# A planned four-layer graph network on one core: transposes in TensorE's planned gaps, fewer one-column products, and wider lags between the layers

## The chip, the core and the metric

The kernel runs on one core of a Trainium2 chip. A core has five engines that each work through a queue of their own, in order: TensorE (PE, matrix products and transposes), VectorE (DVE), ScalarE (ACT), GpSimd (POOL) and SyncE (SP, which here only issues DMAs). They wait for each other through semaphores. The metric is the device time of one execution in microseconds. Before the change it was 1075.67 us, the median of three runs (1072.64 to 1078.02).

## What is computed

The input x is 32 batches of 512 nodes with 128 features; adj is one 512x512 matrix of zeros and ones, shared by all batches. Four graph layers follow each other, each on a normalized copy of x and with a residual:

```python
h = jnp.maximum(_layernorm(x, axis=-1), 0.0);  x = x + L0(h, adj, ...)
h = jnp.maximum(_layernorm(x, axis=-1), 0.0);  x = x + L1(h, adj, ...)
h = jnp.maximum(_layernorm(x, axis=-1), 0.0);  x = x + L2(h, adj, ...)
h = jnp.maximum(_layernorm(x, axis=-1), 0.0);  x = x + L3(h, adj, ...)
```

- Layer 0 is an attention whose scores need only a few values per node (the index arithmetic of the reference pairs nodes up), with a softmax over the first axis, plus a product with a second weight.
- Layer 1 is an attention over edges, multiplied by adj, then a normalization, a sum over neighbours, and a small two-layer network with its own normalization.
- Layer 2 is an attention over edges with an ELU behind it.
- Layer 3 multiplies by a fixed 512x512 matrix, the same for all batches: a softmax over the weights e, which are handed out to the edges of adj in the order in which the edges are counted. That matrix is worked out once (the edge numbers come from cumulative sums, done as products).

All is in 32-bit floats.

## The kernel before

All of x stays on the chip (`xs`). A batch in a layer is one *chain* of operations: statistics of a row (L494, L496, DVE), the power that gives the inverse deviation (L508, POOL), the normalization `xn` (L543, POOL), a transpose of four blocks (L405, PE), a ReLU into `hT` (L553, ACT), products with the weights (`proj` L578, or `p` L564), and then what the layer needs. Layers 1 and 2 share `attend`: `prow` (a transpose that repeats a row), score plus mask with the row maximum (L605, DVE), leaky ReLU and exponential (L630, L638, ACT), transposes of y, `pT` (L647 or L398), and the products `po` (L658). Layer 0 has its own form with pairs of scores fetched by small DMAs (`u`), two scaled copies of h (`hs`, `hs2`, L788 and L789, DVE), a difference `hl` (L803, POOL) and the products L817 to L830. Layer 3 has `own` (L952, DVE), `p`, a copy of h (L396, ACT), the products L963 and L967, the addition `yo` (L974) and the store (L975).

Two chains stand beside those of the batches: `prepare` (masks, centred weights, rows) and `prepare_last` (layer 3's matrix: `pn`, `pb`, `pk`, `pg`, `e_at`, `pd`, `offT`).

The order of the work is written by a planner (`Plan`). Each operation is registered with its engine, a length, its inputs and its outputs; `run` then plays the whole program through with these lengths and a fixed delay per engine. At each step it takes, over all engines, the ready operation that can begin first. Among operations of one engine that can begin within `SLACK` of each other it takes the one with the lowest *turn*. The turn of an operation is its chain's begin plus `STRETCH` times the length of the way to it within its chain; the two preparing chains have a first turn and a step for each operation instead (`PREPARED`, `FILLED`). The begin of a chain is the sum of the gaps (`GAPS`, one for each layer) of the chains ahead of it; the first `AHEAD` = 6 gaps are multiplied by `RAMP`. `LAGS` says by how many batches each layer follows layer 0. A chain may run only within a window of 20 chains from the oldest unfinished one, and a chain at `OLD` or more places from the oldest leaves `KEPT` buffer of a room free. The rooms stand for the 8 banks of PSUM and for groups of SBUF buffers. The engines then follow the planned order on the chip, each at its own pace: a queue never overtakes.

Of the kernel before, what the change touches and what calls it, by code (L numbers as in the profile page):

```python
# [28 lines left out]
F32 = mybir.dt.float32  # L29
# [4 lines left out]
AF = mybir.ActivationFunctionType  # L34
ALU = mybir.AluOpType
AX = mybir.AxisListType

P = 128
# [3 lines left out]

WINDOW = 20

OLD, KEPT = 3, 1

AHEAD = 6

# [1 line left out]
PE, DVE, ACT, POOL, SP = "PE", "DVE", "ACT", "POOL", "SP"  # L50
# [6 lines left out]

SLACK = 0.05

STRETCH = 4.0  # L60

PREPARED, FILLED = (40.0, 1.0), (150.0, 1.5)

RAMP = 4.0

GAPS, LAGS = (5.7, 12.9, 7.2, 5.8), (0, 4, 9, 12)


class Room:
# [38 lines left out]
class Plan:  # L108
# [4 lines left out]
    def __init__(self, tc):  # L113
        self.tc = tc
        self.ops = []
        self.chains = []
        self.begin = 0.0

    def chain(self, gap=0.0, beside=None, name=""):

# [32 lines left out]
    def run(self):  # L153
        tc, nc = self.tc, self.tc.nc
        idle = dict.fromkeys(DELAY, 0.0)
        bus = 0.0
        lanes = [0.0] * LANES

        held = {DVE: [], POOL: []}
        ready = {e: [] for e in DELAY}  # L160
        for op in self.ops:
            if not op.missing:
                ready[op.engine].append(op)
        left = [c[0] for c in self.chains]
        normal = [k for k, c in enumerate(self.chains) if c[1] is None]
        order = {k: i for i, k in enumerate(normal)}
        oldest = 0
        last = {}
        traced = nc.cur_bb.bb.instructions
        seen = len(traced)  # L170
        for _ in range(len(self.ops)):
            while oldest < len(normal) and not left[normal[oldest]]:
                oldest += 1
            best = None
            for engine, ops in ready.items():
                could = []
                for op in ops:
                    k = op.chain
                    beside = self.chains[k][1] is not None
                    if not beside and order[k] >= oldest + WINDOW:  # L180
                        continue
                    begin = max(idle[engine], op.ready)
                    if op.transfers:
                        begin = max(begin, lanes[op.transfers - 1])
                    if op.port:
                        for a, b in held[POOL if engine is DVE else DVE]:
                            if a <= begin < b:
                                begin = b
                    new = [s for s in op.slots if s.tile is None]
                    rooms = {}  # L190
                    for s in new:
                        rooms[s.room] = rooms.get(s.room, 0) + 1
                    for room, n in rooms.items():
                        if len(room.free) < n + (room.reserve if beside else KEPT if order[k] >= oldest + OLD else 0):
                            begin = None
                            break
                        begin = max(begin, sorted(room.free)[n - 1])
                    if begin is not None:
                        could.append((begin, op.turn, op))
                if could:  # L200
                    first = min(c[0] for c in could)
                    c = min((c for c in could if c[0] <= first + SLACK), key=lambda c: c[1])
                    if best is None or c[0] < best[0]:
                        best = c
            assert best is not None, "no operation can begin"
            begin, _, op = best
            ready[op.engine].remove(op)
            for s in op.slots:
                if s.tile is None:
                    s.room.free.remove(min(s.room.free))  # L210
                    s.tile = s.room.make(s.name)
            end = begin + op.length
            idle[op.engine] = end
            if op.port:
                piece = op.length / op.port
                held[op.engine] = [(begin + k * piece, begin + (k + 1) * piece - HOLD) for k in range(op.port)]
            done = end + DELAY[op.engine]
            if op.load:
                bus = max(done, bus) + op.load
                done = bus  # L220
            if op.transfers:
                lanes = lanes[op.transfers :] + [done] * op.transfers
            op.emit()
            traced = nc.cur_bb.bb.instructions
            while seen < len(traced):
                ins = traced[seen]
                seen += 1
                if ins.engine in last:
                    tc.add_manual_dep(
                        ins, last[ins.engine].name,  # L230
                        mybir.DependencyInfo(mybir.DependencyClass.NoSync, mybir.DependencyReason.DATA),
                        reason="the plan's order",
                    )
                last[ins.engine] = ins
            left[op.chain] -= 1
            for s in op.slots:
                s.users -= 1
                s.until = max(s.until, done)
                if not s.users:
                    s.room.free.append(s.until)  # L240
            for n in op.after:
                n.missing -= 1
                n.ready = max(n.ready, done)
                if not n.missing:
                    ready[n.engine].append(n)
# [3 lines left out]
def kernel(  # L249
# [28 lines left out]
    nc = tc.nc  # L278
    B, N, F = x.shape
    C = N // P  # L280
# [4 lines left out]
    KE = NE // P  # L285
# [16 lines left out]
    def const(name, shape, dtype=F32):  # L302
        return cp.tile(list(shape), dtype, name=name)
# [6 lines left out]
    banks = Room(8, lambda n: ps.tile([P, C, P], F32, tag="bank", name=n), reserve=2)  # L310
# [7 lines left out]

    plan = Plan(tc)
    op = plan.op  # L320

    def value(r, name):
        return Value(Slot(r, name))
# [112 lines left out]
    edge = []  # L436
# [7 lines left out]
            wide(e.t).bitcast(BF16)[:, 0:N], bias[:, ib, :], 0.0, None, ALU.is_gt), [v_adj[ib]], [e])  # L444
        edge.append(e)

    def count():
        for jb in range(C):
            for hf in range(2):
                for k in range(H):  # L450
                    nc.tensor.matmul(
                        counts.t[:, jb, hf : hf + 1], lhsT=wide(edge[hf * H + k].t).bitcast(BF16)[:, blk(jb)],
                        rhs=one_b, start=(k == 0), stop=(k == H - 1),
                    )

    op(PE, 1.2, count, edge, [counts])

    def no_edges():

# [23 lines left out]
    def dve(length, emit, reads, writes, port=0):  # L483
        op(DVE, length, emit, reads, writes, port=port)
# [569 lines left out]
    def prepare_last():  # L1054
# [14 lines left out]
        def bf_t():  # L1069
            return wide(bf.t)[:, 0 : 2 * P]  # L1070
# [46 lines left out]
                [pn], [v_n])  # L1117
        pb = value(banks, "pb")

        def emit_pb():  # L1120
            for ib in range(C):
                for kb in range(ib + 1):
                    nc.tensor.matmul(
                        pb.t[:, 0, ib : ib + 1], lhsT=bf_t()[:, 0:P] if kb == ib else bf_t()[:, P:],
                        rhs=row_n[:, kb : kb + 1], start=(kb == 0), stop=(kb == ib),
                    )

        op(PE, 2.2, emit_pb, [bf, v_n], [pb])

        def emit_lo():  # L1130
            nc.vector.tensor_copy(row_lo, pb.t[:, 0, 0:C])
# [45 lines left out]
        def e_at_t(t, kb):  # L1177
            return wide(e_at[t][kb].t).bitcast(F32R)
# [1 line left out]
        in_rowT = [*parts(spare, "in_rowT", 1), *parts(spare, "in_rowT", 1)]  # L1180
        pk = value(banks, "pk")

        def emit_pk():
            for kb in range(KE):
                for ib in range(C):
                    nc.tensor.matmul(
                        pk.t[:, 0, kb : kb + 1], lhsT=in_row_t(ib)[:, blk(kb)], rhs=row_lo[:, ib : ib + 1],
                        start=(ib == 0), stop=(ib == C - 1),
                    )

        op(PE, 1.75, emit_pk, [*in_row, v_lo], [pk])
        dve(0.15, lambda: nc.vector.scalar_tensor_tensor(
            first_k, pk.t[:, 0, 0:KE], -1.0, next_k, ALU.mult, ALU.add), [pk, v_next], [v_first])
        for kb in range(KE):
# [18 lines left out]

            op(POOL, 1.4, emit_at, [ge], [v_adiag_rep], port=1)

            def emit_e(kb=kb):
                for t, e in enumerate((e_hi.bitcast(F32), e_lo)):
                    nc.vector.tensor_scalar(e_at_t(t, kb), adiag_rep, e[:, kb : kb + 1], None, ALU.mult)

            dve(0.65, emit_e, [v_adiag_rep, v_terms], [e_at[0][kb], e_at[1][kb]])  # L1220
            pt = value(banks, "pt_row")
            turn_op(lambda k, pt=pt: pt.t[:, k, :], lambda k, kb=kb: in_row_t(k)[:, blk(kb)], in_row, [pt])
            copy_op(ACT, 0.59, lambda kb=kb: wide(in_rowT[kb].t).bitcast(F32R), lambda pt=pt: wide(pt.t),
# [5 lines left out]
        for ib in range(C):  # L1229
# [32 lines left out]

            def emit_div(ib=ib):
                a = offT[:, ib, :]
                nc.vector.reciprocal(rsum3[:, ib : ib + 1], sum3[:, ib : ib + 1])
                nc.vector.tensor_scalar(a, a, rsum3[:, ib : ib + 1], None, ALU.mult)

            dg = value(spare, "dg")

# [7 lines left out]
            op(POOL, 1.25, emit_mask, [v_bias], [share[ib]], port=1)  # L1277
            dve(0.8, emit_first, [pd], [share[ib]])
            op(ACT, 0.8, emit_exp, [], [share[ib]])
            dve(0.5, emit_div, [], [share[ib]])  # L1280
            dve(0.72, emit_diag, [], [share[ib], dg, v_diag[ib]])
        turned3 = [value(banks, "pt_att3") for _ in range(C)]
        for jb, pt in enumerate(turned3):
# [54 lines left out]
```

## Time and profile before

| | |
|---|---|
| median of three runs | 1075.67 us |
| profiled execution | 1077.78 us |
| its span, first to last instruction | 1076.0 us |
| instructions | 24957 |
| PE busy | 1045.5 us, 97% of the span |
| PE weight loads busy | 965.0 us, 90% |
| DVE busy | 871.7 us, 81% |
| POOL busy | 796.4 us, 74% |
| ACT busy | 763.4 us, 71% |
| mean granted TensorE clock | 0.980 |

A product in 32-bit floats is shown as two instructions (two passes), a transpose as one. Busy times of groups overlap where instructions are pipelined, so that the mean of one is more than what it costs in a row of many. The chain that ended last is PE for 85% of the span. The profile gives the granted clock of PE as a share of its full speed; in the first microseconds it says 1.00, though the transposes there take as long as others do at 0.50.

### The profile page before, as it was taken

How to read it: one execution, taken by the hardware profiler on the slowest of the kernel's cores; microseconds unless marked ns; L12 is line 12 of the kernel's file. 1: busy time of each engine (PE TensorE's matmuls, PEld its weight loads, DVE VectorE, ACT ScalarE, POOL GpSimd, SP SyncE). 2: the span in 40 equal slices, each digit the busy share in tenths (PEclk: the TensorE clock that was granted, in tenths of full speed). 3: DMA queues.
4: the chain of work that ended last, by engine and by line, in shares of the span. 5: the costliest groups of instructions: out<-in, count | busy, mean ns of one | idle time of the engine just before them, and what ended most of it. 6: DMA issues, size and time to landing. Idle time of an engine off the chain costs nothing.

```text
span 1076.0 us, 24957 instructions
## 1 busy us (share of the span) xinstructions
PE 1045.5 (97%) x8341; PEld 965.0 (90%) x8341; DVE 871.7 (81%) x3702; ACT 763.4 (71%) x1976; POOL 796.4 (74%) x1176
## 2 busy tenths in 40 slices
PE   6999999999999999999999999999999999999996
PEld 5887789899899999999999999999999999999995
DVE  7798999999887888888888888888788787776562
ACT  4466778887776777787777777777777777776561
POOL 8689756879777778877787787778778777657644
PEclk8698999999999999999999999999999999999998
DMA  7300000000000000000000000000000000000000
GB/s 179 76 11 1 2 2 10 12 12 21 2 21 21 21 21 22 21 1 21 22 21 12 11 12 4 9 11 12 11 11 12 11 11 12 11 11 21 11 26 25
DMA packets 56912, 20.48 MB, mean 19 GB/s; under 512 B 21584, under 2 KB 56272, under 8 KB 56784
## 3 DMA queue, kind: packets, MB, share of 16 engines
q1 hardware_dynamic: 56784, 18.90, 7.2%
q8 instruction: 66, 1.08, 0.4%
q14 instruction: 62, 0.51, 0.2%
HBM read 10.43 MB, written 8.39 MB: 17 GB/s over the span
## 4 chain that ended last, share of the span: by engine, by line
PE 85%; POOL 5%; DVE 5%; issue 2%; ACT 1%; DMA 1%; SPq 0%; POOLq 0%; DVEq 0%; ACTq 0%
PE po L658 20%; PE pt L405 16%; PE po L967 10%; PE pg L894 9%; PE proj L578 7%; PE po L820 5%; PE prow L405 3%; PE p L564 3%; PE po L825 2%; PE px L564 2%; PE pz L564 2%; PE po L963 2%; POOL xn L543 2%; PE po L817 1%; PE po L830 1%
## 5 line engine op out<-in xcount | busy, mean ns | idle before, releaser
L658 PE MATMUL po<-h,pT 128*128 128x128 f32 x2048 | 243.0, 275 | 0.5 <-ACT ginT L396 0.4
L658 PEld LDWEIGHTS po<-h,pT 128*128 128x128 f32 x2048 | 236.0, 192 | 4.3 <-issue 2.6
L543 POOL TENSOR_SCALAR xn<-xs,shift,rstd 128x128 f32<-128x128 f32 x512 | 230.9, 466 | 2.8 <-PE pt L405 1.2
L638 ACT ACTIVATE y<-y,nmax 128x512 f32<-128x512 f32 x256 | 181.7, 714 | 6.8 <-DVE nmax L620 5.2
L508 POOL TENSOR_TENSOR rstd<-ve,mhalf 128x4 f32<-128x4 f32 x160 | 169.7, 1061 | 13.3
L605 DVE CUSTOM_DVE_ANT_0 y<-prow,bias 128x512 f32<-128x512 f32 x256 | 163.2, 682 | 4.1 <-PE prow L405 4.1
L967 PE MATMUL po<-h,offT 128*128 128x128 f32 x1024 | 136.3, 276 | 0.7 <-ACT h L396 0.7
L405 PE MATMUL pt<-ident,y 128*128 128x128 f32 x1024 | 133.8, 275 | 0.5 <-DVE pT L647 0.2
L894 PE MATMUL pg<-adjTe,hg 128*128 128x512 f32 x256 | 130.9, 594 | 0.0
L405 PEld LDWEIGHTS pt<-ident,y 128*128 128x128 f32 x1024 | 116.0, 141 | 12.5 <-issue 6.2
L967 PEld LDWEIGHTS po<-h,offT 128*128 128x128 f32 x1024 | 125.4, 193 | 1.2 <-ACT h L396 1.2
L630 ACT ACTIVATE y<-y,src 128x512 f32<-128x512 f32 x128 | 85.0, 715 | 46.4 <-DVE rmax L605 43.9
L578 PEld LDWEIGHTS proj<-w_ext,hT 128*128 128x128 f32 x768 | 99.4, 197 | 17.7 <-issue 9.0
L494 DVE BATCH_NORM_STATS2 st<-xs 128x6 f32<-128x128 f32 x512 | 109.6, 275 | 4.3 <-DMA xs<-in_x_dram 2.6
L578 PE MATMUL proj<-w_ext,hT 128*128 128x130 f32 x768 | 106.1, 282 | 1.9 <-ACT hT L553 1.7
L553 ACT ACTIVATE hT<-pt 128x512 f32<-128x512 f32 x128 | 73.7, 588 | 32.7 <-PE pt L405 22.3
L939 POOL TENSOR_TENSOR v<-v,rows 128x512 f32<-128x512 f32 x32 | 40.8, 1274 | 71.4 <-DVE v L938 71.4
L945 POOL TENSOR_TENSOR xs<-xs,em 128x512 f32<-128x512 f32 x32 | 41.9, 1309 | 69.4 <-DVE em L944 63.3
L630 ACT ACTIVATE y<-y,h 128x512 f32<-128x512 f32 x128 | 84.6, 713 | 7.3 <-DVE rmax L605 7.2
L405 PE MATMUL pt<-ident,xn 128*128 128x128 f32 x512 | 82.2, 279 | 7.2 <-POOL xn L543 6.2
L647 DVE TENSOR_TENSOR pT<-pt,adjT 128x512 f32<-128x512 f32 x128 | 82.4, 679 | 3.0 <-PE pt L405 2.9
L396 ACT COPY h<-proj 128x260 f32<-128x260 f32 x192 | 65.0, 371 | 20.5 <-PE proj L578 18.1
(193 smaller groups left out, 2270.4 us busy)
## 6 DMA issues: line engine op xcount, KB each, us to landing
xs<-in_x_dram SPq DMA_DIRECT2D x32, 256.0 KB, 4.1
out_dram<-yo SPq DMA_DIRECT2D x32, 256.0 KB, 2.3
u<-h SPq DMA_DIRECT2D x128, 0.5 KB, 1.8
bias<-in_adj_dram SPq DMA_DIRECT2D x4, 256.0 KB, 3.9
wts<-in_L_gnn_W_dram SPq DMA_DIRECT2D x3, 64.0 KB, 4.0
rows<-in_L_gnn_bias_dram SPq DMA_DIRECT2D x2, 64.0 KB, 3.7
wt_o<-L_gnn_others_weight_dram SPq DMA_DIRECT2D x1, 64.0 KB, 2.5
wts<-n_L_gnn_self_weight_dram SPq DMA_DIRECT2D x1, 64.0 KB, 4.0
```

What stands on the lines that cost most here:

```text
L405: nc.tensor.transpose(dst(k), src(k), ident)
L494: nc.vector.bn_stats(st[:, c, :], src(c))
L508: nc.gpsimd.tensor_tensor(rstd.own, ve, mhalf, ALU.pow)
L543: nc.gpsimd.tensor_scalar(xn.t[:, c, :], src[:, c, :], shift.own[:, c : c + 1], rstd.own[:, c : c + 1], ALU.add, ALU.mult,)
L578: nc.tensor.matmul(p[:, c, :], lhsT=column(hT, 2 * k + c), rhs=w_ext, start=True, stop=True)
L605: nc.vector.tensor_tensor_reduce(wide(y[ib].t), wide(prow.t), bias[:, ib, :], 1.0, LOWEST, ALU.add, ALU.max, rmax.own[:, ib : ib + 1],)
L630: nc.scalar.activation(yw, yw, AF.Prelu, alpha=0.2, bias=src()[:, ib : ib + 1])
L638: nc.scalar.activation(yw, yw, AF.Exp, bias=nmax.own[:, ib : ib + 1], accum_out=ssum[0].own[:, ib : ib + 1])
L647: op(DVE, 0.6, lambda ib=ib, pt=pt, pT=pT: nc.vector.tensor_mul(pT.t, pt.t, weights[:, :, blk(ib)]), [pt, *v_weights], [pT])
L658: nc.tensor.matmul(po[ib].t[:, ib, :], lhsT=pT.t[:, jb, :], rhs=h[0].t[:, jb, 0:P], start=(jb == 0), stop=(jb == C - 1),)
L894: nc.tensor.matmul(wide(pg.t), lhsT=hg.t[:, nb, :], rhs=adjTe[:, nb, :], start=(nb == 0), stop=(nb == C - 1))
L967: nc.tensor.matmul(po[ib].t[:, ib, :], lhsT=offT[:, jb, blk(ib)], rhs=h1.t[:, jb, :], start=False, stop=(jb == C - 1),)
```

## The change

- A new constant `PAUSE` = 0.6 and a function `idle_products`: where the planner is about to place a PE operation that begins more than 0.6 us after PE's last one in the plan, and where a PSUM bank is free, it first issues as many transposes of the identity matrix as fit in the planned gap less 0.2, at 0.11 us each, into that bank. Nothing reads them.
- `pb`, the number of edges ahead of each row block, was ten products of one column; now DVE adds up the columns (`before`), and two products of four columns do the rest.
- The counting of edges (16 products) is registered as four operations instead of one, and `pk` (8 products) as two instead of one, both with new lengths.
- `e_at` (four multiplications of 512 columns by a column) and the division of the rows of `offT` (four) move from DVE to ACT.
- `OLD` goes from 3 to 4; the turns are set anew (`STRETCH`, `PREPARED`, `FILLED`, `RAMP`, `GAPS`), and `LAGS` goes from (0, 4, 9, 12) to (0, 6, 12, 16).

```diff
-OLD, KEPT = 3, 1
+OLD, KEPT = 4, 1
...
-STRETCH = 4.0
-
-PREPARED, FILLED = (40.0, 1.0), (150.0, 1.5)
-
-RAMP = 4.0
-
-GAPS, LAGS = (5.7, 12.9, 7.2, 5.8), (0, 4, 9, 12)
+STRETCH = 3.7
+
+PREPARED, FILLED = (27.0, 1.0), (135.0, 1.3)
+
+RAMP = 3.7
+
+PAUSE = 0.6
+
+GAPS, LAGS = (5.3, 12.0, 6.7, 5.4), (0, 6, 12, 16)
...
             begin, _, op = best
+            if op.engine is PE and begin - idle[PE] > PAUSE:
+                wanted = sum(s.tile is None and s.room is self.banks for s in op.slots)
+                if sum(free <= idle[PE] for free in self.banks.free) > wanted:
+                    self.idle_products(begin - idle[PE])
...
+    def idle_products(time):
+        t = banks.make("idle")
+        for _ in range(int((time - 0.2) / 0.11)):
+            nc.tensor.transpose(t[:, 0, :], ident, ident)
...
-    def count():
-        for jb in range(C):
+    for jb in range(C):
+
+        def count(jb=jb):
...
-    op(PE, 1.2, count, edge, [counts])
+        op(PE, 0.3, count, edge, [counts])
...
+        def emit_before():
+            nc.vector.memset(before[:, 0:1], 0.0)
+            for ib in range(1, C):
+                nc.vector.tensor_add(before[:, ib : ib + 1], before[:, ib - 1 : ib], row_n[:, ib - 1 : ib])
+
+        dve(0.4, emit_before, [v_n], [v_before])
+
         def emit_pb():
-            for ib in range(C):
-                for kb in range(ib + 1):
-                    nc.tensor.matmul(
-                        pb.t[:, 0, ib : ib + 1], lhsT=bf_t()[:, 0:P] if kb == ib else bf_t()[:, P:],
-                        rhs=row_n[:, kb : kb + 1], start=(kb == 0), stop=(kb == ib),
-                    )
-
-        op(PE, 2.2, emit_pb, [bf, v_n], [pb])
+            nc.tensor.matmul(pb.t[:, 0, 0:C], lhsT=bf_t()[:, 0:P], rhs=row_n, start=True, stop=False)
+            nc.tensor.matmul(pb.t[:, 0, 0:C], lhsT=bf_t()[:, P:], rhs=before, start=False, stop=True)
+
+        op(PE, 0.44, emit_pb, [bf, v_n, v_before], [pb])
...
-        op(PE, 1.75, emit_pk, [*in_row, v_lo], [pk])
+            op(PE, 0.88, emit_pk, [*in_row, v_lo], [pk])
...
-            def emit_e(kb=kb):
-                for t, e in enumerate((e_hi.bitcast(F32), e_lo)):
-                    nc.vector.tensor_scalar(e_at_t(t, kb), adiag_rep, e[:, kb : kb + 1], None, ALU.mult)
-
-            dve(0.65, emit_e, [v_adiag_rep, v_terms], [e_at[0][kb], e_at[1][kb]])
+            for t, e in enumerate((e_hi.bitcast(F32), e_lo)):
+                op(ACT, 0.59, lambda t=t, e=e, kb=kb: nc.scalar.activation(
+                    e_at_t(t, kb), adiag_rep, AF.Copy, scale=e[:, kb : kb + 1]), [v_adiag_rep, v_terms], [e_at[t][kb]])
...
-                nc.vector.reciprocal(rsum3[:, ib : ib + 1], sum3[:, ib : ib + 1])
-                nc.vector.tensor_scalar(a, a, rsum3[:, ib : ib + 1], None, ALU.mult)
+                nc.scalar.activation(a, a, AF.Copy, scale=rsum3[:, ib : ib + 1])
...
-            dve(0.5, emit_div, [], [share[ib]])
+            dve(0.1, lambda ib=ib: nc.vector.reciprocal(rsum3[:, ib : ib + 1], sum3[:, ib : ib + 1]), [], [share[ib]])
+            op(ACT, 0.59, emit_div, [], [share[ib]])
```

More of the change, by code (lines that the diff above doesn't have):

```diff
@@ L117, in __init__ @@
         self.begin = 0.0
+        self.banks, self.idle_products = None, None
     def chain(self, gap=0.0, beside=None, name=""):
@@ L320 @@
     op = plan.op
+    def idle_products(time):
+        t = banks.make("idle")
+        for _ in range(int((time - 0.2) / 0.11)):
+            nc.tensor.transpose(t[:, 0, :], ident, ident)
+    plan.banks, plan.idle_products = banks, idle_products
     def value(r, name):
@@ L1118, in prepare_last @@
         pb = value(banks, "pb")
-        def emit_pb():
-            for ib in range(C):
-                for kb in range(ib + 1):
-                    nc.tensor.matmul(
-                        pb.t[:, 0, ib : ib + 1], lhsT=bf_t()[:, 0:P] if kb == ib else bf_t()[:, P:],
-                        rhs=row_n[:, kb : kb + 1], start=(kb == 0), stop=(kb == ib),
-                    )
-        op(PE, 2.2, emit_pb, [bf, v_n], [pb])
+        before = const("before", (P, C))
+        v_before = Value()
+        def emit_before():
[3 more added lines that the diff above has]
+        dve(0.4, emit_before, [v_n], [v_before])
+        def emit_pb():
+            nc.tensor.matmul(pb.t[:, 0, 0:C], lhsT=bf_t()[:, 0:P], rhs=row_n, start=True, stop=False)
+            nc.tensor.matmul(pb.t[:, 0, 0:C], lhsT=bf_t()[:, P:], rhs=before, start=False, stop=True)
+        op(PE, 0.44, emit_pb, [bf, v_n, v_before], [pb])
         def emit_lo():
@@ L1181, in prepare_last, with emit_pk @@
         pk = value(banks, "pk")
-        def emit_pk():
-            for kb in range(KE):
+        for kb in range(KE):
+            def emit_pk(kb=kb):
                 for ib in range(C):
```

## The prediction

> **What bounds the kernel now.** I read the page first, then a table of stages, the waits of VectorE (DVE) in the start, and TensorE's (PE's) timeline at both ends.
>
> ```profile
> span 1076.0 us, 24957 instructions
> PE   6999999999999999999999999999999999999996
> PEclk8698999999999999999999999999999999999998
> ```
>
> PE is full except in the first two or three slices and the last. The stages (columns: length, then busy time and count of PE, PE's weight loads, DVE, ACT, POOL, then the granted clock and DMA) say it more sharply:
>
> ```profile
> 14.00:36.00 22.00, 19.29 (x101) 17.03 (x101) 17.38 (x103) 10.69 (x32) 18.22 (x35) 0.66 0.61 140
> 36.00:61.00 25.00, 22.46 (x147) 21.24 (x147) 21.35 (x109) 12.25 (x46) 14.37 (x22) 0.77 0.10 16
> 79.00:90.00 11.00, 8.99 (x42) 7.60 (x42) 7.79 (x25) 5.95 (x14) 10.65 (x18) 0.69 0.07 21
> 90.00:144.00 54.00, 50.73 (x372) 43.49 (x372) 52.34 (x224) 38.08 (x104) 38.50 (x53) 1.00 0.01 2
> 144.00:1018.00 874.00, 873.53 (x7136) 810.18 (x7135) 720.63 (x3029) 657.17 (x1688) 659.66 (x964) 1.00 0.06 14
> 1047.00:1072.00 25.00, 19.11 (x135) 17.13 (x133) 6.53 (x24) 3.40 (x7) 12.67 (x17) 0.86 0.07 22
> ```
>
> From 144 to 1018 us PE never stops and has its full clock: no reordering can shorten that stage, only less PE work, and the change takes next to none. Up to 144 us DVE is the fullest engine (52.34 of 54 from 90 to 144), and PE's clock is at 0.66 to 0.77 in three stretches. What can move is the start and the tail.
>
> **The accounts of before.** Prices of PE from gaps between starts at full clock: a 128-column transpose 0.109 us, an f32 product of 128 columns (two passes) 0.223, one of 256 columns 0.14, one of 512 (two passes) 0.86. Over the built order of before, without waits, that is 1017.4 us. The eighth batch of layer 0 ends its products at about 145.4 us with 103.6 us of such work done: 41.8 us are lost in the start. The last product ends at 1071.9, so 1071.9 - 1017.4 - 41.8 = 12.7 are lost later, and 4.1 follow (the last addition and store): 41.8 + 1017.4 + 12.7 + 4.1 = 1076.0. The run took 1077.8 (1.8 around the span), 2.1 above the median 1075.7.
>
> The 41.8 can be told from DVE. I summed each DVE instruction in the built order at busy time over count of its row (statistics 0.21, row maximum 0.37 or 0.64, 512-column operations 0.68, small ones 0.17), times 0.857, because rows overlap: from the second to the eighth batch of layer 0 the raw sum is 100.5 and DVE was busy 86. Up to the second scaling (hs2) of the eighth batch that is 124.9 us. DVE idled 18.5: 5.4 before 14 us and 13.1 after. 124.9 + 18.5 = 143.4, and PE has 101.6 of work before it: 41.8 again. The idle after 14 us:
>
> ```profile
> DVE row_lo L1131 <- PE pb L1123: 2.6, 1, 2.6
> DVE xs L836 <- PE po L820: 2.4, 2, 1.3
> DVE pT L647 <- PE pt L405: 1.6, 1, 1.6
> DVE y L710 <- PE prow L405: 1.2, 1, 1.2
> DVE e_at L1218 <- POOL adiag_rep L1212: 1.1, 1, 1.1
> ```
>
> Most of it is DVE waiting for a PE at half clock or held by the one-column products, shown next (start, length, engine, line, tiles).
>
> ```profile
> 5.96 1.12 PE L405 MATMUL pt_adj<-ident,bias 128*128 128x128 f32 x4 [1.60 <-DMA bias<-in_adj_dram]
> 7.15 2.80 PE L405 MATMUL pt_adj<-ident,bias 128*128 128x128 f32 x12
> 9.74 0.69 PE L405 MATMUL pt<-ident,xn 128*128 128x128 f32 x4
> 14.04 2.03 PE L405 MATMUL pt<-ident,xn 128*128 128x128 f32 x4 [1.75 <-POOL xn L543]
> 32.20 4.26 PE L1123 MATMUL pb<-row_n,bf 128*128 128x1 f32 x20
> ```
>
> **The change, part by part.**
>
> *Idle transposes.* The built order has 158: 139 ahead of the third batch's products of layer 0 (groups of 34, 8, 30, 5, 6, 6, 11, 18, 5, 16) and 19 just ahead of the last products. Where the plan sees no gap over 0.6, as after the third batch, none stand. Will they hold the clock? The Trainium skill speaks against it twice. "TensorE: Matmul & The Clock Gate", Part 4: PE-mode transpose, says that the full clock does not engage for transposes, which are not counted as activity. Yet the rows above show 12 transposes from 7.15 taking 2.59 to the next start (0.216 each), and the next four 0.53 (0.13 each): a run of almost nothing but transposes released the clock after 3.7 us. By the rule the 139 would cost 139 x 0.216 = 30 us and release nothing; by the row most cost 0.109. The same page (Why this matters for your kernels) calls PE gaps up to about 3 us harmless. Here the gap of 1.75 us before 14.04 is followed by half clock until 20 us. By the rule there is nothing to win; by the trace the half clock is what such gaps cost. I follow the trace on both.
>
> Their price at the front: ident is ready at 2.1 us, so 34 transposes run about 17 at 0.216 and 17 at 0.109, to 7.8 us. The first real transpose (3.91 in before) is behind them, and on DVE the copy wT is behind that, with the edge tests behind wT in its queue. DVE did some 1.7 us of work in that time: +1.7 idle. Eight more end at 8.7, ahead of the adjacency's transposes, which then run at full clock. The group of 30 lies where PE waits for POOL's second xn, which I put at 17 us (two statistics and two powers of 1.06 go ahead of it); it ends by then. The remaining 67 cost 7.3 us of PE. Up to the third batch DVE has 47.7 us of work and some 10 of idle, PE 27 of real work: about 29 of PE's time is spare, and all 139 take 17. DVE's work is the cover; where it is gone locally, they are DVE waits.
>
> *One-column products.* pb: 10 products (20 passes, 4.26 us) become two of four columns (four passes; nearest row pk, 0.12 a pass at full clock: 0.5). In PE's sum 2.2 less 0.4: 1.8 with rounding, so 1015.7. The running sum on DVE adds a memset and three additions at 0.17: 0.5, ahead of pb, whose wait of 2.6 goes. The counts and pk are only cut into four and two pieces, same work: nothing.
>
> *DVE to ACT.* Four e_at and four divisions of 512 columns, 0.70 each (row of L1266), leave DVE: 5.6. ACT gains eight of 0.6 to 0.7; it is busy 12.3 of 25 in 36 to 61. The division adds a handover of about 0.2 per row block; only layer 3 needs it, and the order brings the first layer-3 output after 274 us of PE work (221 before).
>
> *Plan numbers.* Gaps, stretch, filling start and filling step all fall by about 0.93 or less; turns are only compared with each other, so a common factor does nothing. What is left: preparation due earlier (27 against 40 x 0.93 = 37), a shorter ramp, an extra old chain, and the lags 6, 12, 16. More of layer 0 goes ahead, and layer 0 is heavier on DVE (6.3 us a batch by the rows) than on PE (5.5). In the built order, the point with four batches' worth of layer-1 weighting done on DVE comes with ten batches of layer 0 scaled, not eight. Up to there DVE has 133.1 us and PE 106.4, so 26.7 between them, where before's largest was 23.3. These 3.4 us are a real cost.
>
> *DVE idle after.* 5.4 + 1.7 at the front; of 13.1 the five waits shown (8.9) and 0.7 of the small ones go, 3.5 stay; for new stalls I take 5 (in 61 to 144, nearly all at full clock, DVE idled 4.9). Sum 15.6. From below 9 (no new stall, some of the 3.5 gone too), from above 26 (all 67 later transposes on DVE's path, 7.3, and more of layer 0's chains). Start loss: 133.1 + 15.6 - 106.4 = 42.3, against 41.8: a draw, from -6 to +11.
>
> *Tail.* In before:
>
> ```profile
> 1046.63 3.74 PE L658 MATMUL po<-h,pT 128*128 128x128 f32 x32
> 1052.97 0.76 PE L405 MATMUL pt<-ident,xn 128*128 128x128 f32 x2 [2.60 <-POOL xn L543]
> 1056.66 2.07 PE L564 MATMUL p<-wts,hT 128*128 128x128 f32 x8 [1.41 <-ACT hT L553]
> 1059.41 2.01 PE L967 MATMUL po<-h,offT 128*128 128x128 f32 x8 [0.25 <-ACT h L396]
> ```
>
> The last layer-2 products end at T = 1050.3. After T come 11.5 us of PE work (two layer-3 batches, each 4.47 for po, 0.9 for p, 0.44 for pt) and 4.1 of end, but it takes 25.7: 10.1 lost. With lag 16 the built order has two batches' po (8.9) ready to run behind T, then transposes, pt, p and po of the last. The chain from T to the last pt: v 0.7, row 1.3, exp 0.7, em 0.7, xs 1.3, statistics 1.2, power 1.5, xn 1.7, about 1.2 of handovers: 10.3. The two po cover 8.9. Then own and hT 1.6 with pt's end, p 0.9, h 0.9, po 4.47, end 4.1: 22.1, with 14.7 of work and 4.1 of end in it: 3.3 lost, a gain of 6.8 (4 if the clock still falls, 8 if the 1.2 us of small gaps from 1018 to 1047 go as well). The 19 transposes are 2.1 us within waits of about one us each.
>
> **Sum.** 42.3 + 1015.7 + (12.7 - 6.8) + 4.1 = 1068.0; with 1.8 around it 1069.8; 2.1 less for the median: 1067.7. I give 1067.5.
>
> **Rivals.**
> 1. The start gains too: DVE idle 9, tail -8. 1075.7 - 6.1 - 1.7 - 8 = 1060. For it: the waits named are all tied to PE. Against: the 26.7 us are DVE's own work.
> 2. The start eats the tail: longer chains of layer 0 and the transposes leave DVE idle 22 (+6.9), tail -6.8, sum -1.7: 1074. For it: POOL gets as full as DVE (it was 10.65 of 11 in 79 to 90). Against: the half clock is gone.
> 3. Slower: the transposes don't hold the clock and stand in front of work that DVE waits for. All 139 at 0.216: the front group ends at 9.5 (+3.4 on DVE), 97 others 21, less 8 of real gaps: idle 5.4 + 3.4 + 13.1 + 13 = 35 (+20 in the start), tail -4, sum -1.7: 1090. With that tail it is slower from 5 us more DVE idle than my 15.6, and by 0.5% from 11. For it: the skill's rule. Against: the row at 9.74.
>
> **How the numbers follow.** Mine 0.50, rival 1 0.14, rival 2 0.24, rival 3 0.12. A measurement can tell about 0.5%, 5.4 us. Mine is faster except for its upper edge (0.03), rival 2 about the same: faster 0.62, same 0.26, slower 0.12. The range 1058 to 1079 spans rivals 1 and 2 and leaves out rival 3 and some edges.
>
> **What would show it.** Right: granted clock 1.0 from about 6 us to the tail, DVE busy nearly all of 12 to 140, no pb wait, the start's loss still near 42, the wait before the last pt about 1 us, and 22 us from the last layer-2 product to the end. Wrong: half clock after the transposes (or from 60 to 144 us, in gaps that the plan doesn't see), DVE waits for PE in the first 60 us, or PE waits after 200 us, which the order alone can't exclude.

## The result, and the profile after

The changed kernel takes 1064.1 us (median of five runs, 1063.48 to 1064.81), the kernel before 1074.39 in the same comparison (five runs, 1072.15 to 1078.02): ratio 0.990, 95% interval 0.988 to 0.993. That is faster by about 1%, inside the range and 3.4 us below the predicted 1067.5. The profiled execution took 1063.48 us with a span of 1061.6. The three lines of its page that answer to those shown of before:

```profile
span 1061.6 us, 25176 instructions
PE   8999999999999999999999999999999999999998
PEclk9999999999999999999999999999999999999999
```

The clock row has no dip left. The stages of the kernel after (same columns as before):

```profile
14.00:36.00 22.00, 20.05 (x161) 17.38 (x160) 21.58 (x137) 9.33 (x31) 20.22 (x37) 1.00 0.43 96
36.00:61.00 25.00, 23.66 (x188) 21.04 (x189) 23.14 (x151) 16.95 (x62) 23.94 (x44) 1.00 0.33 76
79.00:90.00 11.00, 9.09 (x76) 8.16 (x75) 10.96 (x43) 8.78 (x27) 10.30 (x18) 1.00 0.12 26
90.00:144.00 54.00, 52.96 (x392) 46.35 (x392) 51.53 (x229) 39.94 (x111) 39.48 (x51) 1.00 0.02 2
144.00:1018.00 874.00, 872.86 (x7129) 808.85 (x7129) 728.93 (x3008) 660.82 (x1685) 659.38 (x960) 1.00 0.05 13
```

The granted clock is 1.00 in all of them, and DVE, which idled 4.6 of 22 us and 3.7 of 25 in the first two stages before, is busy nearly all of both (21.58 and 23.14). But the stage from 144 to 1018 is as full as it was, so the gain has to lie at the ends. PE's timeline at the front and at the tail:

```profile
2.16 6.22 PE L332 MATMUL idle<-ident 128*128 128x128 f32 x34 [2.16 <-POOL ident masks.py:199]
8.22 0.27 PE L426 MATMUL pt_w<-ident,wt_o 128*128 128x128 f32 x1
...
1035.75 3.74 PE L673 MATMUL po<-h,pT 128*128 128x128 f32 x32
...
1048.26 0.93 PE L332 MATMUL idle<-ident 128*128 128x128 f32 x7
1049.02 0.60 PE L419 MATMUL pt<-ident,xn 128*128 128x128 f32 x4
1049.46 0.82 PE L332 MATMUL idle<-ident 128*128 128x128 f32 x6
1051.10 1.16 PE L579 MATMUL p<-wts,hT 128*128 128x128 f32 x8 [0.82 <-ACT hT L568]
...
1056.43 1.06 PE L982 MATMUL po<-h,offT 128*128 128x128 f32 x8
```

The last layer-2 products end at T = 1039.3, and the span ends 22.3 us later; before it took 25.7. Between T and the transposes of the last `xn` there now lie two batches of layer-3 products without a gap; before, this stretch held gaps of 2.60, 0.62 and 1.41 us and products at half clock.

I keep three accounts for every kernel below, all at the prediction's prices. **Start loss**: the end of a late layer-0 batch's products with `hs` (L835 here, L820 in the kernel before; the eighth batch or the tenth) less the PE work ahead of it in the built order. **Cover**: the PE work that the built order has between T and the last `xn` transposes. **Tail loss**: the time from T to the end of the last product, less the PE work in it.

| | before | after |
|---|---|---|
| PE work | 1017.4 | 1015.7 |
| start loss | 41.9 | 36.8 |
| cover | 4.7 | 8.9 |
| tail loss | 9.9 | 3.3 |
| other loss, between the two | 2.7 | 1.6 |

The profiled execution of before was one of its slowest (1077.8, where later medians of 23 to 27 runs are 1072.8 to 1074.2), and its mean granted clock of 0.980 is as low as the lowest of 73 later executions (0.980 to 0.993). By medians the gain is 1074.4 - 1064.1 = 10.3. By the accounts 1.7 of it is PE work, 6.6 tail and 1.1 the stretch between; about 1 is left for the start, if what made that one execution long lies in the start. No other execution of before was profiled, so this last figure is an inference.

### The profile page after: what moved, and what is told of

It is laid out like the page before. It is cut to its first block, busy times and chain, and to the rows that moved or that the text cites. A ratio compares the mean times of both kernels' runs of the same rounds, so it can differ in the third digit from the quotient of the medians.

```text
span 1061.6 us, 25176 instructions
## 1 busy us (share of the span) xinstructions
PE 1043.7 (98%) x8483; PEld 964.5 (91%) x8483; DVE 875.3 (82%) x3698; ACT 766.2 (72%) x1984; POOL 795.8 (75%) x1176
## 4 chain that ended last, share of the span: by engine, by line
PE 86%; DVE 8%; POOL 2%; ACT 2%; issue 1%; SPq 1%; DMA 0%; DVEq 0%; POOLq 0%; ACTq 0%
PE po L673 20%; PE pt L419 16%; PE po L982 10%; PE pg L909 10%; PE proj L593 7%; PE po L835 4%; PE prow L419 3%; PE p L579 3%; PE po L978 3%; PE px L579 3%; PE pz L579 2%; PE po L840 2%; DVE st L509 1%; PE po L845 1%; PE po L832 1%
## 5 line engine op out<-in xcount | busy, mean ns | idle before, releaser
L523 POOL TENSOR_TENSOR rstd<-ve,mhalf 128x4 f32<-128x4 f32 x160 | 171.9, 1075 | 13.3
L419 PE MATMUL pt<-ident,y 128*128 128x128 f32 x1024 | 130.9, 274 | 0.5 <-ACT y L653 0.3
L593 PEld LDWEIGHTS proj<-w_ext,hT 128*128 128x128 f32 x768 | 96.7, 191 | 19.1 <-issue 10.3
L593 PE MATMUL proj<-w_ext,hT 128*128 128x130 f32 x768 | 103.4, 276 | 0.7 <-ACT hT L568 0.5
```

Source lines behind the costliest of these rows:

```text
L419: nc.tensor.transpose(dst(k), src(k), ident)
L523: nc.gpsimd.tensor_tensor(rstd.own, ve, mhalf, ALU.pow)
L593: nc.tensor.matmul(p[:, c, :], lhsT=column(hT, 2 * k + c), rhs=w_ext, start=True, stop=True)
```

## The experiments

All use the changed kernel unless an edit says otherwise. My theory at this point was that of the prediction: the tail comes from the order that the lags make, the idle transposes give the clock and with it take the DVE waits out of the start, and wider lags cost the start 3.4 us. The rival was that the clock does nothing and the order does all.

**No idle transposes.**

```diff
-PAUSE = 0.6
+PAUSE = 1.0e9
```

> The changed kernel with its plan as it is, and no idle transposes. If they make the gain by holding the clock, TensorE is at half clock in several stretches of the first 100 us and in the tail, VectorE waits for TensorE there, and the time goes up by 5 to 9 us (1069 to 1073). If the order of the work makes the gain (moved operations, the two layer-3 batches held back for the tail), the time changes by under 2 us, and by the front group of 34 it may even fall by 1.

Measured: 1063.52 us (1062.36 to 1063.85), ratio 0.990 (0.988 to 0.993), the same as with them. The stages of this kernel:

```profile
14.00:36.00 22.00, 15.91 (x95) 13.15 (x96) 21.19 (x128) 9.34 (x32) 21.02 (x39) 0.84 0.47 102
36.00:61.00 25.00, 22.62 (x164) 19.87 (x163) 23.09 (x149) 16.82 (x63) 23.59 (x44) 0.93 0.33 75
90.00:144.00 54.00, 52.96 (x396) 46.47 (x395) 51.52 (x219) 40.61 (x111) 38.66 (x49) 1.00 0.01 1
```

The clock falls to 0.84 and 0.93, PE has 6 us of room in 22 to take it, and DVE is about as busy as in the kernel after (21.19 against 21.58, 23.09 against 23.14). DVE's idle from 14 to 144 us is 5.5 without the transposes and 5.0 with them; in the kernel before it was 13.1. So in this plan the waits that the prediction gave to the clock are gone without it as well. The tail loss is 4.2 without, 3.3 with: 0.9 us is what the tail's transposes save here.

**Without the front group only.**

```diff
-            if op.engine is PE and begin - idle[PE] > PAUSE:
+            if op.engine is PE and begin - idle[PE] > PAUSE and idle[PE] > 3.0:
```

> The changed kernel without the first group of 34 idle transposes (the other groups stay). If that group holds VectorE up (it waited 3.8 us for the transpose behind it): first transpose at 3.9 us, 1 to 2 us faster. If its warm clock is worth as much: the adjacency's transposes run at half clock again, and the time is the same within 1 us.

Measured: 1062.51 us, ratio 0.990 (0.987 to 0.992). PE's timeline at its front:

```profile
3.87 0.45 PE L426 MATMUL pt_w<-ident,wt_o 128*128 128x128 f32 x1 [3.87 <-DMA wt_o<-L_gnn_others_weight_dram]
4.11 1.91 PE L332 MATMUL idle<-ident 128*128 128x128 f32 x8
```

`pt_w` stands at 3.87 instead of 8.22. In the kernel after, DVE pays for that:

```profile
DVE wT L412 <- PE pt_w L426: 3.8, 1, 3.8
```

The tenth batch's products in L835 end at 142.94 us here, at 142.93 without any idle transposes and at 145.18 in the kernel after. The front group costs 2.2 us in these profiles, the other groups of the start neither cost nor gain. The medians (1062.5 against 1064.1) show 1.6, too small for their intervals to part.

**Idle transposes alone, in the kernel before** (the code of the change; the trace has 175 of them).

```diff
+            if op.engine is PE and begin - idle[PE] > PAUSE:
...
+                    self.idle_products(begin - idle[PE])
```

> The kernel before with idle transposes alone (167 of them, where its own plan has gaps). If the clock is the cause: the half clock in the start goes, with VectorE's waits for TensorE, and the time falls by 4 to 8 us; the tail falls by 2 to 3 more, because the chain there runs at full clock, though its order stays. If the order is the cause: within 2 us of before.

Measured: 1071.83 us, ratio 0.998 (0.997 to 0.999). Start loss 38.5, DVE idle 7.5 before 14 us and 7.4 after it (5.4 and 13.1 without), tail loss 8.0 with a cover of 4.7. In the order where DVE waited for PE they save DVE waits and some tail, but by the medians it comes to 0.2%.

**The new lags alone, in the kernel before; the old lags in the changed plan.**

```diff
-GAPS, LAGS = (5.7, 12.9, 7.2, 5.8), (0, 4, 9, 12)
+GAPS, LAGS = (5.7, 12.9, 7.2, 5.8), (0, 6, 12, 16)
```

> The kernel before with the lags 0, 6, 12, 16 alone. Built, it leaves one layer-3 batch behind the last layer-2 products, not two, and VectorE's lead over TensorE in the start rises from 23.3 to 28.1 us. If the lags make the tail's gain: 2 to 5 us less in the tail. If VectorE's work bounds the start: 3 to 5 us more there. Sum about the same or up to 3 us slower.

Measured: 1082.32 us, ratio 1.008 (1.005 to 1.011). Start loss 48.0; cover 4.5, tail loss 9.4.

```diff
-PAUSE = 0.6
+PAUSE = 1.0e9
...
-GAPS, LAGS = (5.3, 12.0, 6.7, 5.4), (0, 6, 12, 16)
+GAPS, LAGS = (5.3, 12.0, 6.7, 5.4), (0, 4, 9, 12)
```

> The changed kernel without idle transposes, with the old lags 0, 4, 9, 12. Built, one layer-3 batch (4.5 us) is left behind the last layer-2 products instead of two (8.9), and VectorE's lead over TensorE in the start falls from 26.7 to 25.4 us. If these two sums carry the time: 3 to 4.5 us more in the tail, 1.3 less in the start, so 2 to 3 us slower than without idle transposes alone (1065 to 1067). If the lags don't matter: the same as it (1063.5).

Measured: 1090.11 us, ratio 1.014 (1.012 to 1.017), slower than both kernels. Start loss 48.5, tail loss 9.4, and 7.7 more between. PE's waits from 14 to 200 us (engine and what waits, what for; us in total, times, longest):

```profile
PE prow L419 <- DVE ls L710: 8.0, 4, 3.4
PE proj L593 <- DVE rmax L620: 2.9, 1, 2.9
```

PE waits for DVE here. Both of these plans, each with one part of the change and not the other, are slower than the kernel before; the second also has the change's new work on `pb` and on ACT, so new turns entirely alone were not run. And the new lags do not give the tail by themselves: with the old turns the plan still puts 4.5 us behind T.

**The old turns with the new lags.**

```diff
-OLD, KEPT = 4, 1
+OLD, KEPT = 3, 1
...
-STRETCH = 3.7
+STRETCH = 4.0
...
-PREPARED, FILLED = (27.0, 1.0), (135.0, 1.3)
+PREPARED, FILLED = (40.0, 1.0), (150.0, 1.5)
...
-RAMP = 3.7
+RAMP = 4.0
...
-PAUSE = 0.6
+PAUSE = 1.0e9
...
-GAPS, LAGS = (5.3, 12.0, 6.7, 5.4), (0, 6, 12, 16)
+GAPS, LAGS = (5.7, 12.9, 7.2, 5.8), (0, 6, 12, 16)
```

> The changed kernel without idle transposes, with the new lags but the old turns (stretch, preparation, filling, ramp, gaps) and the old 3 old chains. Built, one layer-3 batch is left for the tail, VectorE's lead is 26.2 us. If the order's two sums carry the time: 3 to 4.5 us more in the tail, 0.5 less in the start, 1066 to 1067.5. If the earlier preparation also saves waits in the start: 1068 to 1072.

Measured: 1070.66 us, ratio 0.996 (0.994 to 0.998). Cover 4.5 and tail loss 9.7, so 5.5 of the 7.1 us that it loses are in the tail. The start loss, 34.7 in the profile, is that of one of its fastest executions (1067.98). With the work on `pb` and ACT changed too, the new lags and the old turns are thus not slower than the kernel before, as they were there alone.

**The last lag by itself.** Old lags but for the last, 13 for 12:

```diff
-PAUSE = 0.6
+PAUSE = 1.0e9
...
-GAPS, LAGS = (5.3, 12.0, 6.7, 5.4), (0, 6, 12, 16)
+GAPS, LAGS = (5.3, 12.0, 6.7, 5.4), (0, 4, 9, 13)
```

> The changed kernel without idle transposes, with the lags 0, 4, 9, 13. Built, 10.3 us of layer-3 products stand behind the last layer-2 products ahead of the last transposes, and VectorE's lead is 25.4 us. If the two sums carry the time: 1.3 us less in the start and 1 to 2 less in the tail than 1063.5, so 1060 to 1061.5. If only the spread of the layers counts: it lies with the old lags, 1065 to 1067.

Measured: 1073.5 us, ratio 0.999 (0.998 to 1.000). Cover 10.3, tail loss 2.4; start loss 47.5. The tail is gained and the start is lost. Its timeline shows one thing that may be part of the start's loss (start, length, engine, line, operation, tiles):

```profile
102.30 4.57 DVE L1294 TENSOR_TENSOR offT<-offT,dg 128x128 f32<-128x128 f32 x1
102.35 1.29 POOL L902 TENSOR_TENSOR hn<-hn,rows 128x512 f32<-128x512 f32 x1
...
103.60 1.20 POOL L869 TENSOR_TENSOR h<-h,row_p 128x512 f32<-128x512 f32 x1
...
104.75 1.28 POOL L917 TENSOR_TENSOR hgb<-hg,rows 128x512 f32<-128x512 f32 x1
...
105.97 0.74 POOL L855 TENSOR_TENSOR xs<-xs,rest 128x256 f32<-128x256 f32 x1
...
106.78 0.68 DVE L620 CUSTOM_DVE_ANT_0 y<-prow,bias 128x512 f32<-128x512 f32 x1
```

A subtraction of 128x128 values, for which the multiplication of the same shape ahead of it took 0.28, lasts 4.57 us. It ends at 106.87, just behind the fourth of four POOL instructions in a row (106.71), and DVE's next instruction starts only at 106.78. It counts as busy, so nothing shows it in the waits.

**Back to ten `pb` products, and two products alone in the kernel before.**

```diff
-PAUSE = 0.6
+PAUSE = 1.0e9
...
-        op(PE, 0.44, emit_pb, [bf, v_n, v_before], [pb])
+        op(PE, 2.2, emit_pb, [bf, v_n], [pb])
```

(The ten products come back in place of the sum on DVE and the two products. The second kernel is before with the `pb` part of the change.)

> The changed kernel without idle transposes, with the ten one-column products of pb as before (planned at 2.2 us, and 2.2 us of TensorE at full clock). If what pb costs is its own work: 1.8 us more (1065 to 1066). If the long pb in the middle of the start makes VectorE and TensorE wait for each other (with the new lags and the old pb the start lost 48 us): 1070 or more.

> The kernel before with the two products for pb alone. By its own work and the wait of 2.6 us that stands behind it: 3 to 5 us faster. If pb only helps together with the wider lags (start's loss 41.9 with neither, 48 with the lags alone, 34.7 with both): within 2 us of before. Built, VectorE's lead is 25.7 us, against 23.3.

Measured: with the ten products back (and no idle transposes) 1063.01 us, ratio 0.990 (0.986 to 0.993), the same as with two products; the two products alone in the kernel before, 1070.23, ratio 0.997 (0.995 to 0.998). In the old order, where DVE waited 2.6 us for `pb`, 3 us of a median of 1073.2 go; in the changed order the ten products hold up nothing that counts. In the profile of the old order with two products (1070.79) DVE idles 4.3 us from 14 to 144 us, where before's had 13.1, and the clock is 0.77 from 14 to 36: most of before's waits can go without new lags, new turns or idle transposes too. The median fell by 3 us, less than the 6.6 that the start loss lost between these two profiles, and before's was that of a long execution.

**The moves from DVE to ACT undone.**

```diff
-                nc.scalar.activation(a, a, AF.Copy, scale=rsum3[:, ib : ib + 1])
+                nc.vector.reciprocal(rsum3[:, ib : ib + 1], sum3[:, ib : ib + 1])
+                nc.vector.tensor_scalar(a, a, rsum3[:, ib : ib + 1], None, ALU.mult)
```

(`e_at` likewise, and no idle transposes.)

> The changed kernel without idle transposes, with the four e_at products and the four divisions back on VectorE. If VectorE bounds the start and what is ahead on it decides: up to 5.6 us slower (1067 to 1069). By the built order VectorE's largest lead over TensorE grows by only 0.1 us, because it is reached before most of these operations come: then within 1.5 us of 1063.5.

Measured: 1065.24 us (1061.91 to 1065.72), ratio 0.990 (0.988 to 0.993): the ratio of the kernel without idle transposes. In this order 5.6 us of DVE work less show no worth; the 1.7 us between the medians are those of different comparisons, in which before itself took 1074.2 and 1072.8.

**A change of the plan that changes no work.** The start losses followed none of the causes that I had, so this one asks how far they move with an order that has no reason to be better or worse:

```diff
-SLACK = 0.05
+SLACK = 0.06
...
-PAUSE = 0.6
+PAUSE = 1.0e9
```

> The changed kernel without idle transposes, with the planner's tie range at 0.06 instead of 0.05: no operation is added, removed or made longer, only the order shifts. If the start's gain comes from what the change does: the start's loss stays at 34 to 36 us (1062 to 1065). If it hangs on how a particular order falls: the start's loss moves by several us (1066 or more).

Measured: 1070.44 us (1066.91 to 1074.36), ratio 0.996 (0.994 to 0.998): 6.9 us more than the kernel without idle transposes (6.2 by the two ratios to before), and the start loss goes from 34.6 to 43.5. DVE's waits from 14 to 160 us:

```profile
DVE xs L853 <- PE po L845: 2.9, 3, 1.3
DVE xs L851 <- PE po L835: 1.9, 3, 0.8
DVE score_p L412 <- PE pc L1046: 1.6, 1, 1.6
```

Small waits for PE again, as in before, and one DVE instruction of 3.16 us that ends with a run of POOL instructions, as above. The granted clock is also the lowest of the changed plans here, 0.56 from 14 to 36 us and 0.81 from 61 to 79.

That the clock plays no part can't be said from this. In some kernels the executions with a lower mean clock are the longer ones. With `SLACK` 0.06 the six at 0.992 or less took 1070.4 to 1074.4 us and the five at 0.995 or more 1066.9 to 1069.8. Of 73 executions of before, the 12 at 0.984 or less have a median of 1077.4 (1074.2 to 1078.1), the 24 at 0.989 or more one of 1072.3 (1071.1 to 1075.7). With lags 4, 9, 13 twenty executions at 0.987 to 0.992 show no such order. A low clock may lengthen a start, or a start with more waits may leave PE less busy and lower its clock; no run here tells the two apart.

**One more lag in the tail.** If cover decides the tail and the start order stays, lag 17 should beat 16 (no idle transposes are left in this plan):

```diff
-GAPS, LAGS = (5.3, 12.0, 6.7, 5.4), (0, 6, 12, 16)
+GAPS, LAGS = (5.3, 12.0, 6.7, 5.4), (0, 6, 12, 17)
...
-            if op.engine is PE and begin - idle[PE] > PAUSE:
+            if op.engine is PE and begin - idle[PE] > PAUSE and idle[PE] > 500.0:
```

> The changed kernel without idle transposes, with the lags 0, 6, 12, 17: the start's order is that of the changed kernel, and 10.3 us of layer-3 products stand behind the last layer-2 products instead of 8.9. If the cover decides the tail: its loss falls from 4.2 to 1 to 2 us, 1060 to 1061.5. If the last chain's own length does: 1063.5, as without idle transposes.

Measured: 1059.25 us (four runs, 1057.18 to 1061.61), ratio 0.986 (0.983 to 0.989), the fastest of all. Its tail:

```profile
1031.84 3.74 PE L673 MATMUL po<-h,pT 128*128 128x128 f32 x32
...
1045.68 0.60 PE L419 MATMUL pt<-ident,xn 128*128 128x128 f32 x4
...
1047.75 1.16 PE L579 MATMUL p<-wts,hT 128*128 128x128 f32 x8 [0.35 <-ACT hT L568]
...
1054.55 1.06 PE L982 MATMUL po<-h,offT 128*128 128x128 f32 x8
```

The last transposes of `xn` follow T by 10.3 us of PE work with no gap at all, and the one wait left is 0.35. Its clock from 14 to 36 us is 0.69 in the profiled execution, which was the longest of the four and the one with the lowest mean clock (0.989; the others 0.995 to 0.998).

All accounts together. Each start loss, cover and tail loss is that of one profiled execution. The medians are those of several comparisons, in which before took 1072.8 to 1074.4, so that a microsecond between two rows means little:

| kernel | median | start loss | cover | tail loss |
|---|---|---|---|---|
| before | 1074.4 | 41.9 | 4.7 | 9.9 |
| before, two `pb` products | 1070.2 | 35.3 | 4.7 | 10.5 |
| before, idle transposes | 1071.8 | 38.5 | 4.7 | 8.0 |
| before, new lags | 1082.3 | 48.0 | 4.5 | 9.4 |
| after | 1064.1 | 36.8 | 8.9 | 3.3 |
| no front group | 1062.5 | 34.6 | 8.9 | 3.3 |
| no idle transposes | 1063.5 | 34.6 | 8.9 | 4.2 |
| the same, ten `pb` products | 1063.0 | 33.6 | 8.9 | 4.2 |
| the same, `e_at` and division on DVE | 1065.2 | 34.8 | 8.9 | 3.0 |
| the same, `SLACK` 0.06 | 1070.4 | 43.5 | 8.9 | 3.0 |
| the same, old turns | 1070.7 | 34.7 | 4.5 | 9.7 |
| the same, old lags | 1090.1 | 48.5 | 4.5 | 9.4 |
| the same, lags 4, 9, 13 | 1073.5 | 47.5 | 10.3 | 2.4 |
| no idle transposes, lag 17 | 1059.3 | 38.1 | 10.3 | 0.6 |

## Why the prediction was right, and where it was not

**Tail: right, in mechanism and size.** Predicted 22.1 us from T to the end and a gain of 6.8; measured 22.3 and 6.6. (The terms as I listed them add up to 22.3.) That cover is the cause is shown by fourteen kernels: cover of 4.5 to 4.7 goes with a tail loss of 8.0 to 10.5, 8.9 with 3.0 to 4.2, 10.3 with 0.6 to 2.4, whatever lags and turns they have; and with one lag more and nothing else (17 for 16) the loss falls from 4.2 to 0.6. Some of it goes with the clock from T on: at a cover of 8.9 the four kernels with clock 1.00 there lose 3.0 to 3.3, the two with 0.91 lose 4.2; at 4.7 it is 8.0 with 1.00 against 9.9 and 10.5 with 0.84. (With lag 17 it is 1.00 too, so of its 3.6 us about 2.4 are left for the cover.) The chain from T that I summed to 10.3 us took 9.7 in the kernel after, so a cover of 10.3 leaves next to nothing.

**The step "by the trace the half clock is what such gaps cost": right on the clock, failed on its worth in the start.** That transposes alone release the clock was right: the first 34 took 6.06 us to the next start, which is about 22 at 0.216 and 12 at 0.109 (predicted 17 and 17), so the full clock came about 4.7 us after they began, and it stayed at 1.00. The Trainium skill's rule in "TensorE: Matmul & The Clock Gate" (Part 4: PE-mode transpose), that they are not counted, is not what this chip did with 128x128 transposes in 32-bit floats. What failed is the value I gave the clock. Of the 9.6 us of DVE idle that I let go, 2.6 were the wait for `pb` and 1.1 that of `e_at`, whose work moved to ACT; about 5.9 were left for the clock. In the changed plan they are gone without it as well (5.5 us of idle after 14 us against 5.0, with a clock of 0.84 in the first stage and 6 us of 22 in which PE is idle). The stage table of before had a low clock and DVE waits side by side, in a long execution, and I read the one as the cause of the other. I also called DVE the fullest engine up to 144 us, where the table has PE fuller from 14 to 61 (19.29 against 17.38, 22.46 against 21.35). What stays open is the clock's worth in other orders: in the old one idle transposes took 5.7 us of DVE idle out of the profile and 1 us out of the median, and there a lower mean clock goes with a longer execution.

**The front group: mechanism right, size low.** I added 1.7 us of DVE idle before 14 us; it rose by 2.5, from 5.4 to 7.9. DVE waited 3.8 for `pt_w`, which started at 8.22 and not at 7.8, and the tenth batch came 2.2 us later.

**The lags' "3.4 us are a real cost": failed.** The lead of DVE over PE in the built order does not rank the start losses: it is 26.7 with a loss of 34.6, 25.4 with 47.5 and 23.3 with 41.9. In the changed plan the old lags cost the start 13.9 us, and in the old plan the new lags cost 6.1. What stays open is why some orders lose 35 and others 48. Two parts were seen: small waits between DVE and PE, and DVE instructions held by POOL (4.57 us with lags 4, 9, 13, 4.56 with the old lags, 3.16 with `SLACK` 0.06, but also 2.39 in the fastest kernel, with lag 17). They don't add up to the difference, and since a tie range of 0.06 for 0.05 moves the start by 8.9 us, a start loss of one order says little of the parameter that made it.

**The start in sum: near a draw by the medians,** and in part by luck. Predicted 42.3 after against 41.8; the profile says 36.8 against 41.9, and by the medians only about 1 us of that is gain. Predicted DVE idle was 15.6, measured 7.9 + 5.0 = 12.9. Nearly no new stall came, where I had allowed 5; the 4.9 of idle from 61 to 144 that I took as the measure for it lay for 3.2 in 79 to 90, at a clock of 0.69 and not at full clock. The other 2.8 of the 5.5 between 42.3 and 36.8 are left to the sums of DVE's and PE's own work (133.1 and 106.4).

**One-column products and ACT: the work was right, its worth depends on the order.** `pb` takes 0.64 us in two groups and no DVE wait for it is left. In the changed plan it is worth nothing (1063.0 with ten products); alone in the old one it gave 0.35%. The cuts of the counts and of `pk`, and `OLD` by itself, were not undone one by one.

**The 3.4 us of error** (1067.5 to 1064.1): 1.3 are in where I started from, a median of three runs of 1075.7 that was 1074.4 with five (and 1072.8 in the lowest of the later sets). The other 2.1 are gain that I did not have, 10.3 against 8.2: by the accounts 1.1 between the start and the tail, and about 1 in the start.

## What to carry to other kernels

Before giving an engine's low clock a price, ask whether that engine is the one waited for in that stage: in the changed plan clock 1.00 against 0.84 was worth nothing in the start and 0.9 us in the tail. At the end of a program of chained batches, sum the chain behind the last long stage and let the order hold that much independent work behind it; this one number set most of the gain, 6.6 of 10.3 us. Where a planner writes the order, measure a change of a parameter against a neutral one (a tie range, for example), because a single comparison of orders can move by 0.6% for no reason that the change has. And profile more than one execution before you explain a loss: the one profiled here was longer than most.

## What the runs showed of the hardware

- DVE was held by POOL inside an instruction: 0.28 us of work took 4.57 while four POOL instructions with two inputs ran back to back, as if POOL's next one had taken a shared port again each time before DVE got it. The Trainium skill ("SBUF — State Buffer", SBUF: two separate sides) calls the shared pair of ports of DVE and POOL an exclusive lock that is held for a whole instruction, for a DVE operation with two inputs in SBUF against a POOL operation that reads SBUF; the trace agrees in that DVE's instruction has two inputs in SBUF and ends within 0.2 us of the last POOL instruction, as do those of 3.16 and 2.39 us in the two other kernels. It adds that several POOL instructions can pass, and that the profile shows the time as DVE's busy time (887.1 us in that kernel, 873.6 in the one without idle transposes; 4.3 of the difference are this one instruction). No run took the POOL instructions away, so the cause is inferred from the times.
- The full clock came after about 4.7 us of nothing but f32 transposes, and a gap of 1.31 us (11.8 to 13.1 us in the kernel after) did not take it away (granted clock 1.00; products at 0.11 us a pass behind it). The kernel before lost it between 12.3 and 16.8 us, where PE ran four transposes between gaps of 1.75 and 0.69: eight products took 2.10 us behind that stretch and 1.16 ahead of it.
- The kernel after spread over 1.3 us in five runs (1063.5 to 1064.8), the kernel before over 6 to 7. A clock held at 1.00 is not what does it: without idle transposes, at 0.84 and 0.93 in two stages, four runs spread over 1.5, and before with idle transposes (mean clock 0.994 to 0.998) twenty runs over 5.0.
